# Selective-scan kernel: one scan instruction per unit, decays alternating between PSUM and SBUF, and work moved between the vector, scalar and GpSimd engines

## Chip, cores and metric

The kernel runs on one core of one Trainium2 chip. The metric is the device time of the whole program in microseconds (us). Lower is better. The engines are called as in the profile: PE is the matrix engine, PEld its weight loads, DVE the vector engine, ACT the scalar (activation) engine, POOL is GpSimd, and SP is the engine that issues most DMAs. PSUM is the memory that PE writes to, SBUF the larger on-chip memory. POOL's operations in this kernel read and write SBUF alone.

## What is computed

The input x is 8 images of 96 channels and 64 x 64 points, that is 8 sequences of 4096 tokens. Layer 0 is a selective-scan block with 192 inner channels and 16 states, layer 1 a linear attention and a feed-forward block with rounding to fp8 and fp16:

```python
u = group_norm(x)                                   # tokens x 96
xm, z = split(u @ in_proj_w.T)                      # 192 each
xm = silu(causal_conv4(xm) + conv_b)
dt, Bm, Cm = split(xm @ x_proj_w.T)                 # 6, 16, 16
delta = softplus(dt @ dt_proj_w.T + dt_proj_b)
dA  = exp(delta[..., None] * A)                     # channel x state
dBu = delta[..., None] * Bm[:, :, None, :] * xm[..., None]
h   = dA_t * h + dBu_t                              # over 4096 tokens, from h = 0
y   = sum_n(h * C_t) + xm * D
x   = x + layernorm((y * silu(z)) @ out_proj_w.T) * gamma + beta
t   = x + linear_attention(layernorm(x))            # 6 heads, no softmax
out = t + q16(q16(q8(relu_part) @ q8(W2).T) + q8(b2))
# relu_part = relu(q16(q16(q8(layernorm(t)) @ q8(W1).T) + q8(b1)))
```

Each channel and state is a linear recurrence over the tokens. Its factor is called the decay (dA), its addend dbu.

## The kernel before

**Tiling.** The images are taken in 4 pairs, the 4096 tokens in 8 chunks of T = 512, so there are 32 chunks in order. The 192 channels are 3 groups j of 64, the 16 states 4 groups g of 4. A tile of 128 partitions holds 4 states x 32 channels. A unit u (24 in a chunk) stands for one j, one g and one image b of the pair; its tile has two halves h (32 channels each) of 512 tokens side by side, hence 128 x 1024.

**A unit** (`unit`, L711) issues the following:
- the addend dbu of unit u + 3 (`products_b`, L656): POOL multiplies delta*u (du) by the rows of B, both in SBUF; four dbu buffers;
- two scans on DVE (L741), one for each half, each reading its decay from PSUM (tile da, one bank a half), dbu from SBUF and, as its start, the last state of the chunk before (tile state, one column per half; 0.0 in the first chunk of a pair);
- after each scan, the decay of the next unit's same half on ACT (`decay`, L675, Exp with a per-partition scale);
- the product with C: on DVE from PSUM (L763), where PE has spread the rows of C with a selection matrix (`rows_c`, L664, tile cc), or, for 6 units of the 24 (`POOLED`), on POOL (L770) from rows of C that DMAs have spread in SBUF (`rows`, L639, tile c);
- four matmuls per two units that add the products over the states (`sums`, L688, tile y);
- ACT's copy of the last state of each half (L719).

POOL has a product with C at units 4, 5, 12, 13, 20 and 21, all of g = 2.

**Around the units** run generators, whose steps the table `STEPS` (L37) puts at hand-chosen units, before ("part 0") or behind ("part 1") the scan: P (`chain_p`, the projections, Silu and Softplus of the chunk after next), E (`chain_e`, output projection and layer norms), G (group norm statistics of the next pair), W (attention weights of a pair), F0 and F1 (`chain_f`, the feed-forward block nine chunks later). The order written is the order of each engine's queue. At unit 10 (`SILU`) both decays of unit 12 are issued ahead into two other PSUM banks, mp and mE, just before the step of P that applies Silu to two tiles of 128 x 1536.

**Norms.** `norm_stats` (L399) gathers statistics on DVE (L406, L408); their ends are four small POOL operations (L412, L131, L132, L414: minus the mean, plus eps, the power -0.5, times), queued as "norms" and issued at the next unit's start. `normalise` (L418) applies them on ACT. The fp8 casts of the feed-forward block's hidden tiles are on POOL (L1011), queued as "others", issued behind the next scan.

**Activation tables.** Exp, Silu and Softplus need table loads on ACT; in a chunk there are four (1.28 us each).

**The tail.** After the last unit the remaining feed-forward chains run beside one another ("after" in `chain_f`); there DVE does the ReLUs (L1003) and bias adds that ACT does in the loop.

Of the kernel before, what the change touches and what calls it, by code (L numbers as in the profile page):

```python
# [24 lines left out]
POOLED = (4, 5, 12, 13, 20, 21)  # L25
POOLED_G = 2
SILU = 10
# [13 lines left out]
    3: "F1 F0 P | F1 G6",  # L41
    4: "| E",
# [23 lines left out]
def tile_mamba_linear_attention_ffn(  # L66
# [52 lines left out]

    def psum(tag="mp"):  # L120
        return ps_all.tile([128, T], F32, tag=tag, name=tag, bufs=2 if tag in ("cc", "da") else 1)
# [5 lines left out]
    nc.vector.memset(mhalf, -0.5)  # L127

# [270 lines left out]
    def norm_stats(src, n, tag):  # L399

        mv = p2.tile([128, n, 2], F32, tag=f"mv{tag}", name="mv")
        rstd = p2.tile([128, n], F32, tag=f"rs{tag}", name="rs")
        nmr = p2.tile([128, n], F32, tag=f"nm{tag}", name="nm")
        st = p1.tile([128, n, 6], F32, tag=f"st{tag}", name="st")
        for i in range(n):
            nc.vector.bn_stats(st[:, i, :], src[:, i, :])  # L406
        for i in range(n):
            nc.vector.bn_aggr(mv[:, i, :], st[:, i, :])  # L408


        def ends():
            nc.gpsimd.tensor_scalar_mul(nmr, mv[:, :, 0], -1.0)  # L412
            rsqrt(rstd, mv[:, :, 1], 1e-5)
            nc.gpsimd.tensor_mul(nmr, nmr, rstd)  # L414

        return rstd, nmr, later("norms", ends)

    def normalise(dst, src, norm, q):  # L418
        settle(norm[2])
        nc.scalar.activation(  # L420
            dst, src, AF.Identity, bias=norm[1][:, q : q + 1], scale=norm[0][:, q : q + 1]
        )
# [4 lines left out]
    def load_x(p, c):  # L427

        t = p1.tile([C, 2, T + 3], F32, tag="x", name="x")
        h = 3 if c else 0  # L430
        if not c:
            nc.gpsimd.memset(t[:, :, 0:3], 0.0)
        nc.sync.dma_start(
            t[:, :, 3 - h : T + 3],
            x[2 * p : 2 * p + 2, :, c * T - h : (c + 1) * T].rearrange("b c t -> c b t"),
        )
        x_next[p, c] = t

    def chain_p(p, c, s, after):
# [53 lines left out]
        nc.scalar.activation(zs, zs, AF.Silu)  # L493
        yield
# [26 lines left out]
        nc.scalar.activation(delta, delta, AF.Softplus)  # L521
        yield
# [18 lines left out]
    def first_p(s, after):  # L541
# [75 lines left out]

        cs = s["cs"] = p2.tile([128, T], F32R, tag="cs", name="cs")
# [3 lines left out]
        rows(s, "c", 2 * NS, POOLED_G)  # L622
# [16 lines left out]
    def rows(s, to, of, g):  # L639

        t = s[to, g] = p2.tile([128, 2, T], F32, tag=to, name=to, bufs=NG if to == "b" else 1)
        for n in range(NG):
            nc.sync.dma_start(
                t[32 * n : 32 * n + 32],
                s["bd"][of : of + 2 * NS].rearrange("(b n) t -> n b t", b=2)[NG * g + n]
# [4 lines left out]
    def rows_b(s, g):  # L650
        rows(s, "b", 0, g)
# [12 lines left out]
    def rows_c(s, u):  # L664
        j, g, b = where(u)
        if u in POOLED:
            return
# [7 lines left out]
    def decay(s, u, h, bank=None):  # L675
        if ("da", u, h) in s:
            return
        j, g, b = where(u)
        da = psum(bank) if bank else ps_all.tile([128, T], F32, tag="da", name="da", bufs=2)
        s["da", u, h] = da  # L680
        nc.scalar.activation(  # L681
            da, s["dl", j][:, 2 * b + h, :], AF.Exp, scale=aneg[:, 2 * j + h, g : g + 1]
# [28 lines left out]
    def unit(s, prev, nxt, first, u, steps):  # L711
# [4 lines left out]
        if u - 1 in POOLED:  # L716
# [11 lines left out]
        if u - 3 in POOLED and u % 2 == 0:  # L728
            sums(s, u - 3)
        if u % 2 == 0 and (u or prev is not None) and (u - 1) not in POOLED:  # L730
            sums(s if u else prev, (u or NU) - 1)
# [7 lines left out]
        to, v = at(u + 1)  # L739
        for h in range(2):  # L740
            nc.vector.tensor_tensor_scan(  # L741
                hs[:, h, :], s.pop(("da", u, h)), dbu[:, h, :],
                0.0 if first else state["last"][:, u, h : h + 1], ALU.mult, ALU.add,
            )
            if to is not None:
                decay(to, v, h)
# [7 lines left out]
        if u == SILU and (nxt is not None):  # L754
            for h in range(2):
                decay(s, u + 2, h, ("mp", "mE")[h])
# [3 lines left out]
        if u in POOLED:  # L760
            return
# [5 lines left out]
    def pooled(s, u):  # L767
        j, g, b = where(u)
        pr = s["pr", u] = p2.tile([128, 2, T], F32, tag="pq", name="pr")
        nc.gpsimd.tensor_mul(  # L770
            pr, s["hs", u], s["c", g][:, b, :].unsqueeze(1).to_broadcast([128, 2, T])
# [166 lines left out]
    def chain_f(p, c, b, banks, lane=None):  # L938
# [5 lines left out]
        def place(tag, out_tag, bufs):  # L944
# [5 lines left out]
            [128, NK, C], F32, name="x2", **place(f"x2{b}", ("pr", "b")[(lane or 0) % 2], 4)  # L950
# [34 lines left out]
        casts = []  # L985
# [13 lines left out]
        def relu(m):  # L999
# [6 lines left out]
            else:  # L1006
                nc.scalar.activation(h16[m], h16[m], AF.Relu, bias=b1q[:, m : m + 1])
            casts.append(
                later(
                    "others",  # L1010
                    lambda: nc.gpsimd.tensor_copy(h8[0][:, m, :], h16[m], saturate=False),  # L1011
                )
            )
# [15 lines left out]
        for job in casts:  # L1029
            settle(job)  # L1030
# [6 lines left out]
        y16 = p2.tile([C, T], F16, name="y16", **place("y16", "pq", 2))  # L1037
# [73 lines left out]
    waiting.update(norms=[], others=[])  # L1111
    with tc.manual_schedule():
        for u in range(AHEAD):
            products_b(slots[0], u)
        for h in range(2):
            decay(slots[0], 0, h)
        rows_c(slots[0], 0)
        for i, (p, c) in enumerate(chunks):
# [4 lines left out]
            def steps(u, part):  # L1123
                if part == 0:
# [6 lines left out]
                    if nxt is not None and u == NU - 1:  # L1131
                        rows(nxt, "c", 2 * NS, POOLED_G)
# [3 lines left out]
            for u in range(NU):  # L1136
                unit(s, prev, nxt, c == 0, u, steps)
# [4 lines left out]
    s = slots[N - 1]  # L1142
    sums(s, NU - 1)
# [83 lines left out]
```

## Time and profile before

Three runs give 3161.89, 3162.53 and 3166.35 us, the median is 3162.53. The profiled execution is one more; its page tells its span, from the first to the last instruction.

| What | Value |
|---|---|
| median of the runs | 3162.53 us |
| span of the profiled execution | 3160.5 us |
| first scan starts, last scan ends | 69.5 us, 3008.1 us |
| a chunk, later half of the run | 92.8 to 96.0 us |
| scans (L741) | 1536 of 128 x 512, 1205 to 1276 ns each |
| decays (L681) | 1536, 688 ns each |
| products for dbu (L659) on POOL | 768, 2371 ns each |
| products with C on DVE (L763), on POOL (L770) | 576 at 1213 ns, 192 at 2363 ns |
| ACT table loads | 128 in all |
| DMA | 443.75 MB, 140 GB/s |

Busy time is the time in which an engine works on an instruction. A group's row gives line, engine, operation, tiles and shapes, the count, the busy time, the mean length of one, then the idle time of the engine just ahead of them and what ended it. A recorded length runs until the instruction ends, and may hold time in which it was held up.

### The profile page before, as it was taken

To read this page: it belongs to the slowest core of one execution; us is meant where nothing else is said; L and a number is where in the kernel's file an instruction comes from. 1 tells how busy PE (TensorE), PEld (TensorE's weight loads), DVE (VectorE), ACT (ScalarE), POOL (GpSimd) and SP (SyncE) were. 2 spreads that over 40 slices of the span, in tenths; PEclk is the share of its full clock that TensorE was granted. 3 is DMA by queue.
4 is the path that set the end of the run, shared out by engine and by line. 5 is a ranking of instruction groups with operands and counts; after the bars stand their busy time and mean duration, and the time that the engine had idled before them with its cause. 6 is when DMAs were issued, how large, how long until landed. Compare 5 with 4: busy or idle time off the path is not lost. (4 is left out here: it accounts for less than half of the span.)

```text
span 3160.5 us, 35127 instructions
## 1 busy us (share of the span) xinstructions
PE 2469.6 (78%) x9450; PEld 928.7 (29%) x9450; DVE 2935.2 (93%) x4265; ACT 2263.9 (72%) x4360; POOL 2840.7 (90%) x1921
## 2 busy tenths in 40 slices
PE   6787787878787777777777778777888778887777
PEld 2122222222222223222233323222323222332344
DVE  4999999999999999999999999999999999999945
ACT  3666666667677777777777777777877777777656
POOL 2999999999999999999999999999999999999955
PEclk8677777787778888888888877898888888877668
DMA  6655556665555667555667555567565466755322
GB/s 149 152 122 137 134 156 152 160 150 135 141 143 135 138 162 175 146 129 125 141 164 170 141 146 125 137 157 170 146 148 127 124 144 162 169 132 134 95 70 73
DMA packets 253037, 443.75 MB, mean 140 GB/s; under 512 B 37605, under 2 KB 45990, under 8 KB 252838
## 3 DMA queue, kind: packets, MB, share of 16 engines
q1 hardware_dynamic: 247846, 439.40, 56.9%
q10 hardware_dynamic: 4992, 2.11, 0.3%
q8 instruction: 74, 1.21, 0.2%
q14 instruction: 125, 1.02, 0.1%
HBM read 349.11 MB, written 92.27 MB: 140 GB/s over the span
## 5 line engine op out<-in xcount | busy, mean ns | idle before, releaser
L659 POOL TENSOR_TENSOR dbu<-du,b 128x1024 f32<-128x1024 f32 x768 | 1804.6, 2371 | 112.6 <-DVE hs L741 65.5
L741 DVE TENSOR_TENSOR_SCAN hs<-da,state,dbu 128x512 f32<-128x512 f32 x1290 | 1573.5, 1265 | 25.6 <-ACT da L681 24.6
L681 ACT ACTIVATE da<-dl,aneg 128x512 f32<-128x512 f32 x1474 | 1000.6, 688 | 665.4 <-DVE hs L741 644.2
L763 DVE TENSOR_TENSOR pr<-hs,cc 128x1024 f32<-128x1024 f32 x576 | 698.7, 1213 | 35.1 <-DVE hs L741 0.5
L695 PE MATMUL y<-pr,ssum 128*32 128x512 f32 x2816 | 585.1, 831 | 113.3 <-DVE pr L763 113.3
L770 POOL TENSOR_TENSOR pr<-hs,c 128x1024 f32<-128x1024 f32 x192 | 453.8, 2363 | 36.6 <-DVE hs L741 30.4
L459 PE MATMUL mp<-u,wk 96*64 96x512 f32 x1488 | 398.1, 658 | 66.6 <-ACT xm L477 66.4
L671 PE MATMUL cc<-cs,sel 64*128 64x512 f32 x576 | 330.0, 583 | 144.8 <-DVE pr L763 144.4
L671 PEld LDWEIGHTS cc<-cs,sel 64*128 64x128 f32 x576 | 121.6, 215 | 557.3 <-DVE pr L763 296.8
L741 DVE TENSOR_TENSOR_SCAN hs<-da,dbu 128x512 f32<-128x512 f32 x184 | 213.2, 1205 | 17.4 <-POOL dbu L659 9.9
L516 PE MATMUL mp<-dbl,dtT 12*128 12x512 f32 x186 | 158.9, 947 | 56.8 <-ACT cs L506 38.5
L695 PEld LDWEIGHTS y<-pr,ssum 128*32 128x32 f32 x2816 | 87.9, 132 | 380.6 <-DVE pr L763 201.6
L791 PE MATMUL mE<-woT,zs 128*128 128x192 f32 x744 | 146.6, 350 | 66.7 <-ACT t1e L799 45.1
L459 PEld LDWEIGHTS mp<-u,wk 96*64 96x64 f32 x1488 | 97.0, 145 | 293.6 <-issue 156.6
L132 POOL TENSOR_TENSOR rs<-rs,mhalf 128x8 f32<-128x8 f32 (+1 forms) x128 | 173.3, 1354 | 10.7
L791 PEld LDWEIGHTS mE<-woT,zs 128*128 128x128 f32 x744 | 127.3, 200 | 126.8 <-ACT t1e L799 70.5
L703 PE MATMUL y<-xm,dd 128*128 128x512 f32 x192 | 129.2, 760 | 22.4 <-DVE zs L709 21.9
L467 PE MATMUL mp<-u,wz 96*64 96x512 f32 x372 | 137.0, 825 | 4.3 <-ACT xm L485 4.3
L1011 POOL CAST h<-h 128x512 fp8e5<-128x512 f16 x192 | 117.6, 622 | 24.8 <-DVE h L1003 15.8
L719 ACT COPY state<-hs 128x2 f32<-128x2 f32 x736 | 130.1, 181 | 0.2
L420 ACT ACTIVATE o<-x,nm,rs 128x96 f32<-128x96 f32 x256 | 98.6, 455 | 36.4 <-POOL nm L414 34.4
L531 POOL TENSOR_TENSOR du<-delta,xm 128x512 f32<-128x512 f32 x93 | 117.1, 1273 | 0.0
(306 smaller groups left out, 3234.1 us busy)
## 6 DMA issues: line engine op xcount, KB each, us to landing
du<-lu SPq DMA_DIRECT2D x380, 256.0 KB, 5.5
dl<-ld SPq DMA_DIRECT2D x380, 256.0 KB, 7.9
b<-bd SPq DMA_DIRECT2D x512, 128.0 KB, 5.0
lu<-du SPq DMA_DIRECT2D x96, 256.0 KB, 5.7
ld<-delta SPq DMA_DIRECT2D x93, 256.0 KB, 2.4
c<-bd SPq DMA_DIRECT2D x128, 128.0 KB, 4.4
xg<-in_x_dram SPq DMA_DIRECT2D x32, 384.0 KB, 3.8
xr<-in_x_dram SPq DMA_DIRECT2D x32, 384.0 KB, 8.7
```

What stands on the lines that cost most here:

```text
L132: nc.gpsimd.tensor_tensor(out_, out_, mhalf[0 : out_.shape[0], 0 : out_.shape[1]], op=ALU.pow)
L459: nc.tensor.matmul(ps[64 * b : 64 * b + 64, :], lhsT=wk[:, k, 64 * j : 64 * j + 64], rhs=u[:, b, k : k + T], start=(k == 0), stop=(k == 3),)
L467: nc.tensor.matmul(ps[64 * b : 64 * b + 64, :], lhsT=wz[:, 64 * j : 64 * j + 64], rhs=u[:, b, 3 : T + 3], start=True, stop=True,)
L516: nc.tensor.matmul(ps, lhsT=dtT[:, j, :], rhs=dbl[0 : 2 * RANK, :], start=True, stop=True)
L659: nc.gpsimd.tensor_mul(dbu, s["du", j][:, 2 * b : 2 * b + 2, :], s["b", g][:, b, :].unsqueeze(1).to_broadcast([128, 2, T]),)
L671: nc.tensor.matmul(cc, lhsT=sel[64:128, g, b], rhs=s["cs"][64:128, :], start=True, stop=True)
L681: nc.scalar.activation(da, s["dl", j][:, 2 * b + h, :], AF.Exp, scale=aneg[:, 2 * j + h, g : g + 1])
L695: nc.tensor.matmul(s["y"][q : q + 32, :], lhsT=ssum, rhs=pr[:, h, :], start=False, stop=(g == NG - 1),)
L741: nc.vector.tensor_tensor_scan(hs[:, h, :], s.pop(("da", u, h)), dbu[:, h, :], 0.0 if first else state["last"][:, u, h : h + 1], ALU.mult, ...
L763: nc.vector.tensor_mul(pr, hs, s.pop(("cc", u)).unsqueeze(1).to_broadcast([128, 2, T]))
L770: nc.gpsimd.tensor_mul(pr, s["hs", u], s["c", g][:, b, :].unsqueeze(1).to_broadcast([128, 2, T]))
L791: nc.tensor.matmul(ps[:, 2 * k * C : 2 * (k + 1) * C], lhsT=zs[:, j, tok : tok + 128], rhs=woT[:, j].rearrange("p b c -> p (b c)"), start= ...
```

## The change

The diff does the following:
1. **One scan per unit** of 128 x 1024 over both halves. The decays of a unit lie side by side in one tile; the decay at the start of half 1 is 0 (column written once, left out by the Exp: `h:T`), and ACT puts the carried state into the addend there: dbu[:, 1, 0] += a0 * last (`carry`, one column, pointer scale and bias). The first decays a0 are four more two-column Exps for each j and chunk (`first_decays`). Neither is done in the first chunk of a pair.
2. **Two decay tiles**: even units use PSUM (da, two banks), odd units an SBUF tile (ds). Decays are issued two units ahead, behind the scan of the unit that used the tile. The ahead-of-Silu decays in mp and mE are gone.
3. **Norms**: the four POOL operations become Ln(var + eps) and Exp(-0.5 ...) on ACT and one DVE operation for minus mean times root ("shifts", issued behind the scan). `exp_and_ln()` loads one table that has both, after Silu and after Softplus.
4. **fp8 casts** go to ACT in the loop; in the tail they stay on POOL.
5. **POOL's products with C**: 9 units of 24 instead of 6 (u % 8 in 0, 2, 5), each with its own tile of C rows (64 KB DMAs, 12 a chunk instead of 4 of 128 KB), loaded at units 20, 22 and 1; their results share the ring of four pr tiles. The sums are issued at u % 8 = 3, 5 and 0 (twice).
6. One step of F0 moves from unit 3 to unit 4.

```diff
-POOLED = (4, 5, 12, 13, 20, 21)
-SILU = 10
+POOLED = (0, 2, 5)
+ROWS_POOLED = {20: (0, 0), 22: (1, 0), 1: (2, 1)}
-    3: "F1 F0 P | F1 G6",
-    4: "| E",
+    3: "F1 P | F1 G6",
+    4: "| F0 E",
...
+    das = [
+        ps_all.tile([128, 2, T], F32, tag="da", name="da"),
+        const.tile([128, 2, T], F32, name="ds"),
+    ]
...
-        def ends():
-            nc.gpsimd.tensor_scalar_mul(nmr, mv[:, :, 0], -1.0)
-            rsqrt(rstd, mv[:, :, 1], 1e-5)
-            nc.gpsimd.tensor_mul(nmr, nmr, rstd)
+        def power():
+            nc.scalar.activation(rstd, mv[:, :, 1], AF.Ln, bias=eps5)
+            nc.scalar.activation(rstd, rstd, AF.Exp, scale=-0.5)
+        def shift():
+            nc.vector.scalar_tensor_tensor(
+                nmr, mv[:, :, 0], -1.0, rstd, ALU.mult, ALU.mult
+            )
...
+    def decay(s, u):
         j, g, b = where(u)
+        for h in range(2):
+            nc.scalar.activation(
+                das[u % 2][:, h, h:T], s["dl", j][:, 2 * b + h, h:T], AF.Exp,
+                scale=aneg[:, 2 * j + h, g : g + 1],
+            )
+    def first_decays(s, j):
+        a0 = s["a0", j] = p2.tile([128, NG, 2], F32, tag="a0", name="a0")
+        dl = s["dl", j].rearrange("p (b h) t -> p b h t", h=2)
+        for g in range(NG):
+            nc.scalar.activation(
+                a0[:, g, :], dl[:, :, 1, 0], AF.Exp, scale=aneg[:, 2 * j + 1, g : g + 1]
+            )
+    def carry(s, u, last):
+        j, g, b = where(u)
+        if not u % (2 * NG):
+            first_decays(s, j)
+        to = s["dbu", u][:, 1, 0:1]
         nc.scalar.activation(
+            to, s["a0", j][:, g, b : b + 1], AF.Identity, bias=to, scale=last[:, u, 1:2]
         )
...
-        for h in range(2):
-            nc.vector.tensor_tensor_scan(
-                hs[:, h, :], s.pop(("da", u, h)), dbu[:, h, :],
-                0.0 if first else state["last"][:, u, h : h + 1], ALU.mult, ALU.add,
-            )
-            if to is not None:
-                decay(to, v, h)
+        if u + 1 < NU:
+            if not first:
+                carry(s, u + 1, state["last"])
+        elif nxt is not None and not last:
+            carry(nxt, 0, state["new"])
+        nc.vector.tensor_tensor_scan(
+            hs.rearrange("p h t -> p (h t)"),
+            das[u % 2].rearrange("p h t -> p (h t)"),
+            dbu.rearrange("p h t -> p (h t)"),
+            0.0 if first else state["last"][:, u, 0:1], ALU.mult, ALU.add,
+        )
+        to, v = at(u + 2)
+        if to is not None:
+            decay(to, v)
+        now("shifts")
         now("others")
...
-        if u in POOLED:
+        if u % 8 in POOLED:
             return
...
-            casts.append(
-                later(
-                    "others",
-                    lambda: nc.gpsimd.tensor_copy(h8[0][:, m, :], h16[m], saturate=False),
-                )
-            )
+            if after:
+                nc.gpsimd.tensor_copy(h8[0][:, m, :], h16[m], saturate=False)
+            else:
+                nc.scalar.activation(h8[0][:, m, :], h16[m], AF.Copy, saturate=False)
```

## The prediction

> **What bounds the kernel now.** I read the busy times first, then the stretch in which the scans run (first scan at 69.5 us, last end at 3008 us), then the waits.
>
> ```profile
> PE 2469.6 (78%) x9450; PEld 928.7 (29%) x9450; DVE 2935.2 (93%) x4265; ACT 2263.9 (72%) x4360; POOL 2840.7 (90%) x1921
> ```
>
> ```profile
> 69.00:3005.00 2936.00, 2311.26 (x8796) 838.61 (x8796) 2829.49 (x3874) 2149.80 (x4113) 2742.39 (x1722) 0.81 0.59 144
> ```
>
> ```profile
> ACT da L681 <- DVE hs L741: 644.2, 820, 4.0
> ...
> POOL dbu L659 <- DVE hs L741: 65.5, 66, 2.6
> ...
> DVE hs L741 <- ACT da L681: 31.7, 43, 1.2
> ```
>
> The second fence is the table of busy times by stretch: length, then PE, PEld, DVE, ACT, POOL. In these 2936 us DVE works 2829 (96.4%), POOL 2742 (93.4%), ACT 2150 (73%). The waits agree: ACT waits 644 us for scans, POOL 65 us, the scans hardly for anyone. DVE bounds, POOL is 3% behind. The chain that ended last covers only some 1% of the span (the tail) and says nothing of the loop. Outside this stretch lie 3160.5 - 2936 = 224.5 us. My sums are made against the span of 3160.5; the median of the runs is 3162.5, so I add 2 at the end.
>
> **The rows that price the parts** (by form: shapes, count | busy, mean ns).
>
> ```profile
> L659 POOL TENSOR_TENSOR dbu<-du,b 128x1024 f32<-128x1024 f32 x768 | 1804.6, 2371 | 112.6 <-DVE hs L741 65.5 <-DMA ld<-delta 36.9 <-DMA dl<-ld 4.6
> L741 DVE TENSOR_TENSOR_SCAN hs<-da,state,dbu 128x512 f32<-128x512 f32 x1290 | 1573.5, 1265 | 25.6 <-ACT da L681 24.6
> L763 DVE TENSOR_TENSOR pr<-hs,cc 128x1024 f32<-128x1024 f32 x576 | 698.7, 1213 | 35.1 <-DVE hs L741 0.5
> L770 POOL TENSOR_TENSOR pr<-hs,c 128x1024 f32<-128x1024 f32 x192 | 453.8, 2363 | 36.6 <-DVE hs L741 30.4 <-DMA xr<-in_x_dram 3.6 <-DMA xg<-in_x_dram 1.4
> L709 DVE TENSOR_TENSOR zs<-y,zs 128x512 f32<-128x512 f32 x96 | 64.2, 668 | 5.4 <-PE y L695 4.7
> L132 POOL TENSOR_TENSOR rs<-rs,mhalf 128x8 f32<-128x8 f32 x64 | 106.8, 1670 | 5.3
> ```
>
> *One scan of 1024 for two of 512.* A pair costs 1573.5/1290 x 2 = 2.44 us of DVE. A longer scan is not in the trace. At worst nothing is gained: 2.44. What doubling saves is one fixed part: the products show it, 2 x 668 (L709) - 1213 (L763) = 123 ns; the pointer start (scans with state 1259, without 1199 at the median) may save another 60: 2.26. I take 2.30, near the 123 ns: 768 x 0.14 = -107 us on DVE.
>
> *Products with C.* 96 move (288 instead of 192 on POOL): DVE -96 x 1.213 = -116, POOL +96 x 2.36 = +227. PE loses 96 spreads of C (L671), which bound nothing.
>
> *Norms.* A norm on POOL is four operations: L412 257, L131 248, L132 1670, L414 205 ns at 8 columns (2.38 us), 1.73 us at 4. Of the 128 norms some 21 lie in the tail; the others take 226 us from POOL. DVE gets one small operation each (L186 is like it, 130 ns): +14. ACT gets Ln and Exp: about 0.28 and 0.18 us (L681 less its 512 columns; the small copy L719, 181 ns), 107 x 0.46 = +49. Both lie in one table, and by the instruction order the table loads stay 63 + 31 + 31: no new load.
>
> *Casts.* 138 go to ACT at L997's 578 ns: +80 there; 132 of them, in the loop, leave POOL: -132 x 0.612 = -81.
>
> *Carry.* 672 one-column operations with pointer scale and bias: L420 takes 455 ns for 96 columns; at the 0.79 ns a column of 674 (512) to 1483 (1536) it is 0.38 us, so +255. 336 first decays of two columns: 0.28 us, +95. ACT in all: 2150 + 479 = 2629.
>
> *Waits on ACT.* A carry waits for POOL's product of the same unit; behind it in ACT's queue stand the decays of the unit after, copies and norms, and the scans wait for them. POOL runs up to three units ahead, which covers it; where POOL is late, the scan waits for that product anyway, so it adds nothing. And a carry stands behind Silu with its loads (1.28 + 1.48 + 1.47 + 1.28 = 5.5 us). Before, both decays of unit 12 were made ahead in two spare banks; now, after unit 10's scan, ACT does two decays (1.4), Silu (5.5), state and carry (0.6): 7.5 us, while DVE has one scan, one product and some 0.5 to do (4.0). That is up to 3.5 us a chunk, 31 x 3.5 = 108 us, on DVE if DVE has no other wait.
>
> *Rows of C.* 12 loads of half the size for 4 a chunk, on SP, which waits 463 us in all for one chain alone. They are issued four to five units (15 us and more) ahead of their readers, c landed in 4.4 us; their old readers are POOL products three units back. Nothing waits behind them: 0. The later sums are 8 short matmuls a chunk-third instead of 4 ahead of the gate, under a scan of 2.3 us: 0.
>
> Without anything else DVE comes to 2829 - 107 - 116 + 14 = 2620, POOL to 2742 + 227 - 226 - 81 = 2662, ACT to 2629: three level engines.
>
> **The port.** What the sum leaves out is where the decays lie. They alternate between PSUM (even units) and an SBUF tile "ds" (odd units). An odd scan then streams both operands from SBUF; no scan of before does (its POOL neighbours never stretch: L659 2338 to 2452 ns). How DVE and POOL can meet in SBUF, the trace shows in three places (timeline: start, us, operation):
>
> ```profile
> 606.12 2.36 POOL L659 TENSOR_TENSOR dbu<-du,b 128x1024 f32<-128x1024 f32 x1 [1.96 <-DMA dl<-ld]
> ...
> 606.50 2.00 DVE L170 COPY gnm<-gnmv 96x2 f32<-96x2 f32 x1
> ...
> 608.42 1.21 DVE L763 TENSOR_TENSOR pr<-hs,cc 128x1024 f32<-128x1024 f32 x1
> ```
>
> ```profile
> 3032.07 0.61 POOL L1011 CAST h<-h 128x512 fp8e5<-128x512 f16 x1 [0.92 <-DVE h L1003]
> ...
> 3032.24 0.58 DVE L1003 TENSOR_SCALAR h<-h,b1q 128x512 f16<-128x512 f16 x1
> ```
>
> ```profile
> 622.08 1.67 POOL L132 TENSOR_TENSOR rs<-rs,mhalf 128x8 f32<-128x8 f32 x1
> ...
> 622.88 0.16 DVE L176 TENSOR_TENSOR gndev<-gnm,gnmean 96x2 f32<-96x2 f32 x1
> ```
>
> A copy of two columns, 165 ns when POOL is idle, lasts 2.00 us and ends 0.02 us after the POOL product at 608.48; its two later sisters in the loop also end with a POOL product. L1003 (330 ns alone) ends 0.14 us behind POOL's cast. So DVE and POOL can shut each other out for a whole instruction. The third fence is the other bound: operations with two SBUF inputs passed beside POOL's power unhindered (nine of nine). But L1003 passes beside the power too (0.35 us at 3071.13, inside a power of 1.04 us from 3071.09), so that operation keeps nobody out, and the nine tell little. No long POOL operation meets a two-input DVE operation in this trace: what an odd scan costs POOL lies between 0 and its full length. Its neighbours are POOL's long products, as in the first fence, so I take the exclusive end as the nearest row, and POOL pays: 384 x (2.30 + 0.03) = 895; the 107 norm shifts, two SBUF inputs too, 107 x 0.16 = 17. POOL with what it is shut out: 2662 + 895 + 17 = 3574 us. DVE waits for half a POOL product (1.2) per odd scan or shift: 2620 + 491 x 1.2 = 3209, so it has room, and the 108 us behind Silu fit into it. At a bound engine's share between 96.4% (now) and 100%, 98%: 3647; + 224.5 + 2 = **3874, say 3870 us**. With 2.26 a scan and 100% it is 3785; with 2.44 and 96.4%, 3990.
>
> A rule speaks to just this. The Trainium skill, "SBUF — State Buffer", section "Who interferes with whom", says that a DVE instruction with two SBUF inputs contends with a GpSimd instruction that reads SBUF, through the shared read interface, and that the loser blocks fully. By it the sum is the 3870 above; by the third fence alone, taken as the rule's counterexample, it would be the 3050 below. No run here shows it for a scan.
>
> **The rivals.**
> *No contention.* Then the change is faster: DVE 2620 + 108 behind Silu = 2728, POOL 2662. At 96.4%: 2830 + 224.5 + 2 = **3055** (3000 to 3155, as three level engines with ACT one unit ahead may reach less). It decides from the price of an odd scan on POOL: the loop keeps its 2936 us when POOL holds 0.98 x 2936 = 2877, that is (2877 - 2662)/384 = 0.56 us a scan; below that the change is faster, above it slower. For it: L176 to L178; against: L170, L1003.
> *Port shared, not locked.* Both read at once and slow one another; half the exclusive price, 448: POOL 3110 / 0.97 = 3206, **3430** (3160 to 3780).
> *ACT becomes the bound without contention.* 2629 at 88% (waits for scan, product and Silu in one queue): 2988 + 227 = **3215**, on the slow side by a little. In the level state this needs ACT to lose 12%; now it loses 27%, but for lack of work.
> *The scan doesn't shrink.* At 2.44 a scan DVE has 107 more: 3055 becomes 3160; under the lock it adds 54 (384 x 0.14).
>
> **How the numbers follow.** Lock 0.68, shared 0.11, no contention and faster 0.17, ACT-bound or level 0.04 (of which within 0.2%: 0.02). 0.2%, some 6 us, is about what a measurement of this kernel can tell from no change. Faster 0.17, same 0.02, slower 0.81. The lock's own range is 3785 to 3990, with 0.65 of chance. To hold 8 in 10 the range takes in the shared port and the slow ACT case and leaves out the faster one: 3160 to 3990.
>
> **What would show it.** Lock: POOL products of du and b stretched to 4 us and more, or DVE scans on ds with a recorded time far above those on da; POOL's busy share near 100%; ACT and DVE idle behind dbu. No lock: all these products stay at 2.37 us and scans of both tiles at 2.3. Silu: scan of unit 12 late by some 3 us in each chunk. I am wrong if both scan forms take the same 2.3 us beside unstretched POOL products.

## The result, and the profile after

The changed kernel takes 3689.23 us (median of four runs, 3686.88 to 3692.76), the kernel before on the same chip 3162.21 us (four runs): a ratio of 1.166, interval 1.1646 to 1.1679. The profiled execution spans 3687.5 us. The forecast was 3870 us, the range 3160 to 3990.

The busy times of the changed kernel:

```profile
PE 2676.0 (73%) x9610; PEld 1039.6 (28%) x9610; DVE 3336.0 (90%) x3532; ACT 2658.3 (72%) x5762; POOL 3417.5 (93%) x1367
```

The table by stretch, from its first scan (72.3 us) to the end of its last (3558.7 us); the columns are the stretch, its length, PE, PEld, DVE, ACT and POOL:

```profile
72.00:3558.00 3486.00, 2531.97 (x8970) 962.33 (x8970) 3230.01 (x3119) 2535.99 (x5469) 3362.17 (x1261) 0.72 0.50 124
```

POOL works 3362 of these 3486 us (96.4%, before 93.4%), DVE 3230 (92.7%, before 96.4%). DVE executes fewer instructions than before and is still busy for 400 us more, so part of its "busy" must be waiting inside instructions. The groups show where:

```profile
L689 POOL TENSOR_TENSOR dbu<-du,b 128x1024 f32<-128x1024 f32 x768 | 2195.7, 2879 | 60.7 <-DMA du<-lu 36.8
L793 DVE TENSOR_TENSOR_SCAN hs<-ds,state,dbu 128x1024 f32<-128x1024 f32 x336 | 1135.3, 3379 | 28.6 <-ACT dbu L728 24.7
L823 POOL TENSOR_TENSOR pr<-hs,c 128x1024 f32<-128x1024 f32 x288 | 852.6, 2961 | 73.2 <-DVE hs L793 35.0
L793 DVE TENSOR_TENSOR_SCAN hs<-da,state,dbu 128x1024 f32<-128x1024 f32 x336 | 786.1, 2339 | 70.6 <-ACT dbu L728 61.0
...
L728 ACT ACTIVATE dbu<-a,dbu,state 128x1 f32<-128x1 f32 x672 | 255.9, 381 | 70.9 <-POOL dbu L689 70.7
...
L428 DVE SCALAR_TENSOR_TENSOR nm<-mv,rs 128x8 f32<-128x8 f32 (+1 forms) x128 | 154.1, 1204 | 40.4 <-ACT rs L425 39.2
```

The even scans, which read their decay from PSUM (da), take 2339 ns. The odd ones have the same shape and count and read it from SBUF (ds): 3379 ns. The kernel's granted TensorE clock is lower too (0.72 against 0.81 in the stretch of the scans), but that cannot be what makes the odd scans longer: the even ones run at the same clock. POOL's product for dbu has grown from 2371 to 2879 ns, its product with C from 2363 to 2961 ns. A carry costs 381 ns. The shift of the norms (L428), a few columns wide, takes 1204 ns. The timeline shows what a meeting of the two engines looks like, in two places, and at the end a scan on da for comparison (start, length, operation):

```profile
1499.64 6.66 POOL L689 TENSOR_TENSOR dbu<-du,b 128x1024 f32<-128x1024 f32 x2
1499.73 4.41 DVE L793 TENSOR_TENSOR_SCAN hs<-ds,state,dbu 128x1024 f32<-128x1024 f32 x1
...
1518.58 2.32 DVE L793 TENSOR_TENSOR_SCAN hs<-ds,state,dbu 128x1024 f32<-128x1024 f32 x1
...
1518.80 4.26 POOL L823 TENSOR_TENSOR pr<-hs,c 128x1024 f32<-128x1024 f32 x1 [1.25 <-DVE hs L793]
...
1523.02 2.34 POOL L689 TENSOR_TENSOR dbu<-du,b 128x1024 f32<-128x1024 f32 x1
...
1523.17 2.35 DVE L793 TENSOR_TENSOR_SCAN hs<-da,state,dbu 128x1024 f32<-128x1024 f32 x1 [0.56 <-ACT dbu L728]
```

First the scan begins 0.09 us behind a product and lasts 4.41 us, until 1504.14: it is held while the product runs, then takes its 2.3 us, and the second product behind it is held in turn (6.66 us for two that need 4.7). In the second place the scan is first by 0.22 us; it takes 2.32 us, and the product, held until about the scan's end, takes 4.26 us. The last two lines show a scan on da beside a product: neither is longer than its group's usual 2.34 and 2.36 us.

Summed over the trace, POOL's operations in this stretch are 698 us longer than their undisturbed lengths (dbu 403, products with C 174, the rest 121), that is 1.82 us for each of the 384 odd scans; a product that is stretched at all is stretched by 2.0 us for dbu and 1.7 for C. The odd scans are 405 us longer than even ones. Without these, POOL has 3362 - 698 = 2664 us of work.

The waits of the changed kernel (who waited for whom: us in all, times, longest) carry little beside that (ACT waits most, for scans, and is not the bound at 72%):

```profile
ACT ds L708 <- DVE hs L793: 411.3, 216, 7.5
...
ACT dbu L728 <- POOL dbu L689: 70.7, 84, 3.1
...
DVE hs L793 <- ACT dbu L728: 85.7, 92, 3.4
DVE nm L428 <- ACT rs L425: 39.2, 28, 2.1
```

Of the 85.7 us that scans wait for the carry, 48 lie at unit 12, behind Silu (24 of 32 chunks, 2.0 us each).

### The profile page after: what moved, and what is told of

Same layout as the page of the kernel before. It is cut to its first block, busy times and chain, and to the rows that moved or that the text cites. A ratio compares the mean times of both kernels' runs of the same rounds, so it can differ in the third digit from the quotient of the medians.

```text
span 3687.5 us, 35488 instructions
## 1 busy us (share of the span) xinstructions
PE 2676.0 (73%) x9610; PEld 1039.6 (28%) x9610; DVE 3336.0 (90%) x3532; ACT 2658.3 (72%) x5762; POOL 3417.5 (93%) x1367
## 5 line engine op out<-in xcount | busy, mean ns | idle before, releaser
L689 POOL TENSOR_TENSOR dbu<-du,b 128x1024 f32<-128x1024 f32 x768 | 2195.7, 2879 | 60.7 <-DMA du<-lu 36.8
L793 DVE TENSOR_TENSOR_SCAN hs<-ds,state,dbu 128x1024 f32<-128x1024 f32 x336 | 1135.3, 3379 | 28.6 <-ACT dbu L728 24.7
L823 POOL TENSOR_TENSOR pr<-hs,c 128x1024 f32<-128x1024 f32 x288 | 852.6, 2961 | 73.2 <-DVE hs L793 35.0
L793 DVE TENSOR_TENSOR_SCAN hs<-da,state,dbu 128x1024 f32<-128x1024 f32 x336 | 786.1, 2339 | 70.6 <-ACT dbu L728 61.0
L708 ACT ACTIVATE da<-dl,aneg 128x512 f32<-128x512 f32 (+1 forms) x768 | 529.3, 689 | 390.0 <-DVE hs L793 358.9
L708 ACT ACTIVATE ds<-dl,aneg 128x512 f32<-128x512 f32 (+1 forms) x768 | 511.2, 713 | 412.4 <-DVE hs L793 411.3
L816 DVE TENSOR_TENSOR pr<-hs,cc 128x1024 f32<-128x1024 f32 x480 | 581.5, 1212 | 25.9 <-DVE hs L793 0.9
L728 ACT ACTIVATE dbu<-a,dbu,state 128x1 f32<-128x1 f32 x672 | 255.9, 381 | 70.9 <-POOL dbu L689 70.7
L428 DVE SCALAR_TENSOR_TENSOR nm<-mv,rs 128x8 f32<-128x8 f32 (+1 forms) x128 | 154.1, 1204 | 40.4 <-ACT rs L425 39.2
L793 DVE TENSOR_TENSOR_SCAN hs<-ds,dbu 128x1024 f32<-128x1024 f32 x48 | 166.1, 3460 | 11.0 <-POOL pr L823 7.8
```

The costliest lines, as they stand in the source:

```text
L689: nc.gpsimd.tensor_mul(dbu, s["du", j][:, 2 * b : 2 * b + 2, :], s["b", g][:, b, :].unsqueeze(1).to_broadcast([128, 2, T]),)
L708: nc.scalar.activation(das[u % 2][:, h, h:T], s["dl", j][:, 2 * b + h, h:T], AF.Exp, scale=aneg[:, 2 * j + h, g : g + 1],)
L728: nc.scalar.activation(to, s["a0", j][:, g, b : b + 1], AF.Identity, bias=to, scale=last[:, u, 1:2])
L793: nc.vector.tensor_tensor_scan(hs.rearrange("p h t -> p (h t)"), das[u % 2].rearrange("p h t -> p (h t)"), dbu.rearrange("p h t -> p (h t) ...
L816: nc.vector.tensor_mul(pr, hs, s.pop(("cc", u)).unsqueeze(1).to_broadcast([128, 2, T]))
L823: nc.gpsimd.tensor_mul(pr, s["hs", u], s["c", g, b].unsqueeze(1).to_broadcast([128, 2, T]))
```

## The experiments

Times are medians; a ratio is to the kernel before, in runs on the same chip. Theory L is the prediction's: DVE and POOL shut each other out whenever a scan reads both operands from SBUF. Its rivals are that new waits in the queues make the time, or that DVE bounds anyway. Other letters hold within one text only.

**1. The lock by itself.** Pairs of a DVE and a GpSimd operation, by themselves. Tile pa lies in PSUM, all others in SBUF; the two stretches below stand for seven.

```diff
+        for _ in range(N):
+            nc.vector.tensor_tensor_scan(h, pa, b, 0.0, ALU.mult, ALU.add)
+            nc.gpsimd.tensor_mul(r, p, q)
+        fence()
+        for _ in range(N):
+            nc.vector.tensor_tensor_scan(h, a, b, 0.0, ALU.mult, ALU.add)
+            nc.gpsimd.tensor_mul(r, p, q)
...
```

> The kernel leaves the whole computation out and writes constants; it only runs stretches of twelve pairs, one DVE and one GpSimd operation at 128x1024 that share no data. Theory L (the lock: a DVE operation whose two operands both lie in SBUF and a GpSimd operation that reads SBUF shut each other out for whole instructions): the scan from PSUM beside the GpSimd product keeps 2.3 us and the product 2.36 us; the scan with both operands in SBUF beside the product makes a pair of 4.5 to 4.8 us (12 pairs in about 56 us); beside a GpSimd memset, which reads nothing, it keeps 2.3 us; beside a GpSimd multiplication by a constant, which reads one operand, it is shut out as well; a DVE product of two SBUF operands is shut out like the scan (pair of some 3.6 us), a DVE product from PSUM is not (2.36 us); the operation of 8 columns waits for the end of the product each time (2.0 to 2.4 us recorded). Rival S (the port is shared, both run slower at once): pairs of 2.4 to 4 us with both operations stretched, and the 8-column operation takes well below 1 us. Rival N (the long scans of the changed kernel are slow for another reason, say dependences): every pair takes the longer of its two, about 2.4 us.

The groups of this kernel by shape, costliest first. Pairs stand on neighbouring lines: L136 with L137, L140 with L141, and so on; p, q, a, b are in SBUF, pa in PSUM:

```profile
L141 POOL TENSOR_TENSOR r<-p,q 128x1024 f32<-128x1024 f32 x12 | 50.7, 4221 | 0.9
L140 DVE TENSOR_TENSOR_SCAN h<-a,b 128x1024 f32<-128x1024 f32 x12 | 49.0, 4083 | 0.4
L153 POOL TENSOR_TENSOR r<-p,q 128x1024 f32<-128x1024 f32 x12 | 38.6, 3219 | 0.9
L152 DVE TENSOR_TENSOR h<-a,b 128x1024 f32<-128x1024 f32 x12 | 36.9, 3075 | 0.4
L149 POOL TENSOR_SCALAR r<-p 128x1024 f32<-128x1024 f32 x12 | 36.7, 3055 | 1.0
L148 DVE TENSOR_TENSOR_SCAN h<-a,b 128x1024 f32<-128x1024 f32 x12 | 34.6, 2886 | 0.4
L161 POOL TENSOR_TENSOR r<-p,q 128x1024 f32<-128x1024 f32 x12 | 28.2, 2346 | 0.9
L157 POOL TENSOR_TENSOR r<-p,q 128x1024 f32<-128x1024 f32 x12 | 28.1, 2343 | 0.9
L137 POOL TENSOR_TENSOR r<-p,q 128x1024 f32<-128x1024 f32 x12 | 28.1, 2340 | 0.9
...
L144 DVE TENSOR_TENSOR_SCAN h<-a,b 128x1024 f32<-128x1024 f32 x12 | 27.5, 2290 | 0.4
...
L136 DVE TENSOR_TENSOR_SCAN h<-pa,b 128x1024 f32<-128x1024 f32 x12 | 27.5, 2290 | 0.4
L156 DVE TENSOR_TENSOR h<-pa,b 128x1024 f32<-128x1024 f32 x12 | 14.7, 1223 | 0.4
L160 DVE SCALAR_TENSOR_TENSOR h<-a,b 128x8 f32<-128x8 f32 x12 | 14.2, 1180 | 0.4
L145 POOL MEMSET r<- 128x1024 f32 x12 | 11.4, 951 | 0.7
```

Beside the scan from PSUM (L136) the product keeps 2340 ns, as alone (2338); beside the same scan from SBUF (L140) both become 4.1 to 4.2 us long. So the effect needs no other part of the kernel, and rival N falls. That it is a lock and not a port shared at half speed (S) shows in the shortest and longest of a group (ns: shortest, median, longest):

```profile
L140 DVE TENSOR_TENSOR_SCAN h<-a,b x12: 2278/4246/4250, 124.4 to 169.5; 128x1024 f32<-128x1024 f32 x12
...
L160 DVE SCALAR_TENSOR_TENSOR h<-a,b x12: 154/1180/2195, 312.5 to 324.8; 128x8 f32<-128x8 f32 x12
```

The first SBUF scan, which starts with the first product (within 0.01 us), takes 2.28 us as alone, and that product 4.42; the 8-column operations take up to 2.19 us. A memset, which reads nothing, is no partner (L144). A DVE product of two SBUF operands is shut out like the scan (L152). A GpSimd operation that reads one operand makes the scan 0.6 us longer (L148, 2886 ns); how long that operation (L149) takes alone was not run, so whether the two shut each other out for the whole length, as was expected, is not shown. But two exclusive operations would need 2.29 + 2.34 = 4.63 us a pair and take 4.22: some 0.4 us overlap, and POOL loses 4.22 - 2.34 = 1.88 us a scan, not 2.33. The 8-column operation takes 1180 ns on average: every second one waits to the end of the product (2.19 us), the next passes in 0.17, and POOL loses nothing.

**2. The place of the operand alone.** The kernel before, two scans of 512 kept, with the decays of odd units in SBUF.

```diff
-        da = psum(bank) if bank else ps_all.tile([128, T], F32, tag="da", name="da", bufs=2)
+        if u % 2:
+            da = p2.tile([128, T], F32, tag="ds", name="ds", bufs=2)
+        else:
+            da = psum(bank) if bank else ps_all.tile([128, T], F32, tag="da", name="da", bufs=2)
```

POOL's results go through the ring of DVE's here too, to make room.

> The kernel before, with one thing changed: the decays of the odd units lie in SBUF, those of the even units stay in PSUM. There are still two scans of 512 a unit; norms, casts and the six products on GpSimd stay (the latter's results use the ring of the other products, which makes room). Theory L (an odd scan reads two SBUF streams and shuts GpSimd out, and waits for it): GpSimd's 2742 us in the loop grow by 768 half scans x 1.26 us x 0.78 (the share that the changed kernel showed: 698 us for 384 scans of 2.33) = 755; 3497 at 96.4% and 222 outside: 3850 us, 3500 to 3900; products on GpSimd stretched in bundles. Rival W (GpSimd or ScalarE simply got too much work in the change): no work moves here, so 3160, within 15.

3963.43 us, ratio 1.253 (1.251 to 1.2547): moving the operand alone costs 800 us against the kernel before on the same chip (3163.75 us), more than the whole change. Its page, the busy times and three groups:

```profile
PE 2843.6 (72%) x9450; PEld 1014.3 (26%) x9450; DVE 3724.6 (94%) x4265; ACT 2242.4 (57%) x4360; POOL 3339.1 (84%) x1921
...
L659 POOL TENSOR_TENSOR dbu<-du,b 128x1024 f32<-128x1024 f32 x768 | 2021.1, 2644 | 313.6 <-DVE hs L744 274.1
L744 DVE TENSOR_TENSOR_SCAN hs<-ds,state,dbu 128x512 f32<-128x512 f32 x672 | 1497.5, 2267 | 15.7 <-ACT ds L684 14.6
...
L744 DVE TENSOR_TENSOR_SCAN hs<-da,state,dbu 128x512 f32<-128x512 f32 x618 | 755.6, 1263 | 0.0
```

A half scan on ds takes 2267 ns instead of 1263: 768 x 1.004 = 771 us of waiting on DVE, which is 94% busy and bounds. POOL loses 498 us (3339 - 2841). That scans and products hold each other up, as L says, holds; but L laid the loss on POOL (755 us more), and here it is DVE that loses most and bounds. Its range (up to 3900) was too low, because each of the 768 half scans can wait anew. A half scan waits as long as a whole one does in the changed kernel (1.0 and 1.05 us), so here the price on DVE goes by the number of meetings, not by the length.

**3. One scan a unit alone.** The kernel before with the long scan, the carry and ds (parts 1 and 2 of the change, with the step of F0 that moves); norms, casts and 6 of 24 products as before, their results in the ring of DVE's.

```diff
+        nc.vector.tensor_tensor_scan(
+            hs.rearrange("p h t -> p (h t)"),
+            das[u % 2].rearrange("p h t -> p (h t)"),
+            dbu.rearrange("p h t -> p (h t)"),
+            0.0 if first else state["last"][:, u, 0:1], ALU.mult, ALU.add,
+        )
...
```

> The kernel before with the one scan per unit alone (decays in PSUM and SBUF by turns, carries and first decays on ScalarE); norms, casts and six products stay on GpSimd. Theory L: GpSimd's 2742 us grow by 384 x 1.8 = 700; 3440 at 96.4% and 222 outside: 3790, 3650 to 3850 us. If the loss came from the other parts: 3060 to 3200.

3791.08 us, ratio 1.196 (1.1943 to 1.1979). Its busy times:

```profile
PE 2796.0 (74%) x9450; PEld 1008.4 (27%) x9450; DVE 3309.0 (87%) x3499; ACT 2520.9 (67%) x5368; POOL 3586.9 (95%) x1921
```

POOL goes from 2840.7 to 3586.9 us of busy time, 746 more, 1.94 us for each odd scan, and is 95% busy; L's number is met. The part alone costs 623 us against the kernel before on the same chip (3168.53 us), more than all parts together (527).

**4. Everything but the one scan.** The changed kernel with two scans of 512, decays in PSUM and the ahead-of-Silu decays, as before.

```diff
-        nc.vector.tensor_tensor_scan(
-            hs.rearrange("p h t -> p (h t)"),
...
+        for h in range(2):
+            nc.vector.tensor_tensor_scan(
+                hs[:, h, :], s.pop(("da", u, h)), dbu[:, h, :],
+                0.0 if first else state["last"][:, u, h : h + 1], ALU.mult, ALU.add,
+            )
+            if to is not None:
+                decay(to, v, h)
...
```

> The changed kernel with two scans of 512 a unit and all decays in PSUM as before; norms and casts on ScalarE, nine of 24 products on GpSimd. Theory L: no long stretch; GpSimd 2664, DVE 2829 - 116 + 107 norm shifts x (0.13 + up to 1 of waiting) = 2750 to 2840; at 96.4% and 205 outside: 3060 to 3150, faster than before by 0.5 to 3%. Rival W: GpSimd overloaded by the products as in the change, 3500 or more.

3339.94 us, ratio 1.055 (1.0529 to 1.0569). No stretched product (POOL's dbu 2364 ns), and yet 190 us above what was expected. So the scans on ds are not the whole loss: the other parts are slower by themselves, by 176 us against the 527 of the whole change. Three waits of it:

```profile
POOL pr L793 <- PE y L715: 127.0, 50, 5.1
POOL dbu L679 <- DVE hs L763: 115.0, 61, 3.6
DVE nm L418 <- ACT rs L415: 109.4, 54, 2.8
```

DVE waits 109 us for roots at the head of its queue, where before none of these was; the shift itself has 77.2 + 48.7 = 126 us for 128 operations that need 0.13 us each. POOL waits 127 us for the sums that free the ring of four.

**5. Norms alone, with the shift on DVE and on GpSimd.** The kernel before with Ln and Exp on ACT. In the second version the shift stays on GpSimd:

```diff
-            nc.vector.scalar_tensor_tensor(
-                nmr, mv[:, :, 0], -1.0, rstd, ALU.mult, ALU.mult
-            )
+            nc.gpsimd.tensor_scalar_mul(nmr, mv[:, :, 0], -1.0)
+            nc.gpsimd.tensor_mul(nmr, nmr, rstd)
```

> The kernel before with the norms alone changed: roots as Exp of Ln on ScalarE, the shift as one DVE operation with two SBUF inputs. Theory S: each of some 107 shifts in the loop costs DVE about 1 us at the port and 0.9 us of waiting for ScalarE's roots: DVE 2829 + 200; 3250 to 3380 us. By the prediction's price without waits (14 us on DVE, GpSimd 226 less): 3150 to 3180.

> The kernel before with the norms' roots on ScalarE (Ln, Exp) and their two small operations left on GpSimd: the norms' part of the change without the shift on DVE, everything else as before. Moving the norms with the shift on DVE measured 3260 us, 97 more than before. Theory S (the price lies in the shift: an operation at the head of DVE's queue that waits for a root in ScalarE's queue, and for GpSimd's port): without it DVE, 2829 us of work, bounds as before: 3155 to 3175 us, GpSimd down to some 2560. Rival Q (the price lies in ScalarE's queue, where decays now stand behind roots that wait for DVE's statistics): it stays at 3210 to 3260, with scans waiting for decays.

3259.79 us, ratio 1.0283 (1.0267 to 1.0298), with the shift on DVE; 3157.65 us, ratio 0.998 (0.9972 to 0.999), with it on GpSimd. The group of the shift, from the page of the version with the shift on DVE:

```profile
L418 DVE SCALAR_TENSOR_TENSOR nm<-mv,rs 128x8 f32<-128x8 f32 (+1 forms) x128 | 90.6, 708 | 31.8 <-ACT rs L415 31.8
```

Two waits of the version with the shift on GpSimd:

```profile
POOL nm L419 <- ACT rs L415: 51.9, 38, 2.7
...
DVE hs L753 <- ACT da L693: 34.1, 46, 2.1
```

One small operation on the bound engine, 128 times, costs about 100 us (102 by the two medians, 96 by the two ratios). The first fence accounts for them: 90.6 us in which the 128 shifts hold DVE, where 128 x 0.13 = 17 were priced, and 31.8 us of idle time ahead of them, waiting for a root: 74 + 32 = 106. That they last 708 ns on average (1146 at 8 columns) agrees with the 8-column pairs of experiment 1 (1180). With the shift on GpSimd the wait for the root (51.9 us) falls on POOL, which has the room. The roots on ACT cost nothing (34 us of scans waiting for decays, 32 before), and POOL's 205 us less work (2635.6 against 2840.7) is worth about 6 us, since DVE bounds. This version is faster than both kernels, than the one before by 0.2%.

The same swap in the version of experiment 4:

> The kernel with all of the change but the one scan, and the norm shift made by two GpSimd operations (minus the mean, times the root) instead of one DVE operation. Theory S: DVE loses the 218 us of waiting of that kernel's 3340, GpSimd gains 50: 3060 to 3180 us, at or below before. Rival Q (the ring of four result tiles, for which GpSimd waited 127 us there, or the order of the queues bounds): 3280 to 3350.

3259.32 us, ratio 1.0284 (1.0254 to 1.0313), 81 us less than with the shift on DVE. It lies between the two ranges of the text, a little under Q's. Here scans wait 130 us for ACT's decays and POOL 116 us for the sums, so the shift is one part of what was missed in experiment 4. The queue of ACT and the ring are, by these waits, the rest; neither was tried alone.

**6. Products alone, and a version without two SBUF reads on DVE's long operations.** The first is the kernel before with the 9 of 24 products. The second is the last version of experiment 5 (3259.32 us) with 8 products of 24, a ring of five, and the casts on GpSimd again; the lines below leave out those of the casts:

```diff
-POOLED = (0, 2, 5)
+POOLED = (0, 2, 5, 8, 13, 16, 18, 21)
...
-        pr = s["pr", u] = p2.tile([128, 2, T], F32, tag="pr", name="pr", bufs=4)
+        pr = s["pr", u] = p2.tile([128, 2, T], F32, tag="pr", name="pr", bufs=5)
...
```

> The kernel before with one part of the change alone: three of eight products with C on GpSimd, spread, with own tiles for the rows of C; the norms, casts and both scans a unit stay as before. By the terms of the prediction GpSimd gets 96 x 2.36 = 227 us more, 2742 + 227 = 2969, and becomes the bound: at 96.4% to 100% 2969 to 3080 + 224.5 = 3190 to 3305 us; DVE falls to 2713. Rival R (the ring of four results that GpSimd and DVE now share, with sums three units later, adds waits of DVE on the sums): DVE and GpSimd both below 93% busy and above 3330 us. If GpSimd were not the bound: 3050 us.

> A version that keeps what pays: two scans of 512 from PSUM as before (no decays in SBUF), the norms' roots on ScalarE with their shift on GpSimd, casts on GpSimd again, eight products of 24 with C on GpSimd, in a ring of five. By the rows DVE has 2829 - 64 x 1.213 = 2751 us, GpSimd 2742 + 151 - 180 = 2713, ScalarE 2150 + 49 = 2199: if the engines keep the level of before, 2751/0.964 + 222 = 3076 us. If the waits that the version of nine products showed come from the ring of four and from the casts in ScalarE's queue, it comes to 3060 to 3150. Rival Q: the waits come from the roots in ScalarE's queue (decays stand behind a root that waits for DVE's statistics); then it stays at 3200 to 3280, above the kernel before.

3318.82 us, ratio 1.0486 (1.047 to 1.0501), and 3201.33 us, ratio 1.0118 (1.0101 to 1.0135). The products alone make POOL the bound, a little above the top of the expected 3305: of the 3096 us from 69 to 3165 POOL works 2961 (95.6%). The second is 58 us better than the last version of experiment 5 but 50 above what was expected, just inside Q's range. Its waits:

```profile
POOL pr L792 <- DVE hs L762: 87.9, 67, 2.3
...
POOL dbu L678 <- DVE hs L762: 69.7, 84, 3.6
DVE hs L762 <- ACT da L700: 66.8, 56, 4.8
DVE gram L890 <- PE mE L881: 62.2, 20, 3.6
```

DVE at 90% and POOL at 87% wait for each other, for ACT's decays and for PE in turn, none for long. Since three edits went into it together, it doesn't tell which of them gave the 58 us.

**7. Two of eight products on POOL.** The changed kernel with one product of each eight back on DVE:

```diff
-POOLED = (0, 2, 5)
-ROWS_POOLED = {20: (0, 0), 22: (1, 0), 1: (2, 1)}
+POOLED = (0, 5)
+ROWS_POOLED = {20: (0, 0), 1: (2, 1)}
...
```

> The changed kernel with two of eight products with C on GpSimd instead of three (units 0 and 5 of each eight). Theory L with GpSimd as the bound: its loop of 3362 loses 96 x 2.36 = 227, 3135 at 96.4% and 201 outside: 3450 us (3420 to 3520), still far above before. Rival A (ScalarE's queue, the carries behind Silu, is what bounds): unchanged, 3690 within 20. Rival D (DVE, with its waits at the port, bounds): slower, by 96 x 1.21 = 116, some 3800.

3603.93 us, ratio 1.1398 (1.1379 to 1.1417). Its busy times:

```profile
PE 2664.9 (74%) x9706; PEld 1048.1 (29%) x9706; DVE 3268.6 (91%) x3628; ACT 2652.4 (74%) x5762; POOL 2925.9 (81%) x1271
```

It fits none of the three. 96 products fewer are 227 us less for POOL and 116 more for DVE; the time falls by 85. POOL is 81% busy, DVE 91%, the odd scans take 3031 ns instead of 3379. So a loop in which POOL bounds alone does not describe it. One reading is that under the lock neither engine bounds alone: what one gives up the other partly takes by running into it. No run tests that reading by itself.

**8. Taking the lock out of the changed kernel: two tries that brought waits of their own.** The first has three PSUM banks for the decays, for which C's spread rows keep one bank instead of two and the decays come later. The second lets odd scans read one zero column of PSUM instead of ds. Their edits, one behind the other:

```diff
-    das = [
-        ps_all.tile([128, 2, T], F32, tag="da", name="da"),
-        const.tile([128, 2, T], F32, name="ds"),
-    ]
+    da3 = ps_all.tile([128, 3, T], F32, tag="da", name="da")
+    das = [da3[:, 0:2, :], da3[:, 1:3, :]]
...
-        cc = s["cc", u] = ps_all.tile([128, T], F32, tag="cc", name="cc", bufs=2)
+        cc = s["cc", u] = ps_all.tile([128, T], F32, tag="cc", name="cc", bufs=1)
...
```

```diff
-            das[u % 2].rearrange("p h t -> p (h t)"),
+            das[0][:, 1, 0:1].to_broadcast([128, 2 * T])
+            if u % 2 else das[0].rearrange("p h t -> p (h t)"),
```

> The changed kernel with all decays in PSUM: three banks side by side, even units in banks 0 and 1, odd units in banks 1 and 2; the spread rows of C have one bank instead of two. One decay of the next unit can start only after the scan, and ScalarE has one small copy more per even unit (a zero in the shared bank). Theory L: GpSimd's products go back to 2.36 us each, its loop to 2664, DVE to some 2640 plus waits for the late decay (up to 0.8 us in 3 of 8 units): 3050 to 3250 us. Rival W (too much work on GpSimd or ScalarE): the work is the same and ScalarE has 75 us more, so 3690 or more.

> The changed kernel; its odd scans read, in place of the decays in SBUF, one zero column of PSUM repeated 1024 times, so the recurrence of the odd units is left out. ScalarE still makes those decays, every instruction of every queue stays, and only the odd scan's second SBUF stream is gone. Theory L (the two-stream scan shuts GpSimd out): scans of both kinds 2.3 us, GpSimd's products 2.36 us each, but for the norm shifts; its loop back to some 2680. With L alone as the loss, 3050 to 3150; with theory S beside it (the norm shift on DVE waits for ScalarE's roots and at the port, as the kernel without the one scan showed: 3340), 3150 to 3350. If the port is not the cause: 3690.

3758.57 us, ratio 1.188 (1.1863 to 1.19), and 3498.49 us, ratio 1.104 (1.102 to 1.1057). In both the stretching of products and scans is gone (POOL's dbu 2358 and 2363 ns, scans of even and odd units some 2345), but both are slow for a reason that is not in the changed kernel. Two waits of the first:

```profile
ACT da L710 <- DVE hs L793: 476.0, 298, 4.4
DVE hs L793 <- ACT da L710: 434.2, 418, 3.8
```

And one of the second:

```profile
DVE hs L793 <- ACT da L708: 252.9, 252, 2.4
```

The first makes a circle of decay and scan, in which each waits for the other 434 and 476 us. In the second the zero column belongs to the tile da, so odd scans wait for the next even unit's decays (253 us). For theory L both expectations missed. The first time lies where its rival W put it (3690 or more), but not for W's reason of too much work: POOL and ACT are 73% busy. The two versions show that the stretching comes from ds, and don't give the time of a changed kernel without the lock.

## Why the prediction was right, and what in it was not

- **The range held with some luck.** The lock's own range, 3785 to 3990, was missed from below: 3689 lies in the range that the prediction gave for a shared port (3160 to 3780), and only the whole range took both in. So the time alone does not tell a lock from a shared port; the timelines and experiment 1 do.
- **The lock** was the likeliest case, and holds: with the operand in PSUM no product is stretched (experiments 1, 4 and 8), with it in SBUF they are, and its place alone costs 800 us (2). The rule of the Trainium skill that the prediction weighed ("SBUF — State Buffer", section "Who interferes with whom") agrees with the rows of experiment 1 in who meets whom: of the DVE operations there only those with two SBUF inputs, and only beside a POOL operation that reads. That the loser waits out the whole instruction holds there beside a POOL product, but for 0.3 to 0.4 us, and is open beside the POOL operation with one operand. Experiment 1 has no copy; in the first fence of the prediction's part on the port a copy with one SBUF input is held as well (2.00 us), so two inputs are not the only case. The third fence there, the nine small operations that passed beside the power, did not decide it; why they passed was not tried.
- **The shut-out was mis-sized**: 895 + 17 us on POOL in the prediction (2.33 us a scan, 0.16 a shift), 698 measured (1.82 a scan, shifts included). Experiment 1 shows 1.88 us a scan for POOL, since about 0.4 us of each pair overlap, and a shift costs POOL nothing. This is the largest error: (912 - 698)/0.98 = 218 us.
- **POOL without shut-outs**: 2662 predicted, 2664 measured. One scan of 1024: 2.30 predicted, 2.34 (da) measured. The carry: 255 and 256 us. First decays: 95 and 72 us.
- **POOL's share** was taken as 98% and is 96.4% (+57 us), and outside the loop lie 201 us, not 224.5 (-24). With -218 these make the 185 us between 3874 and 3689.
- **DVE** was put at 3209 us with its waits and has 3230, but the step "so it has room" was too easy: at 92.7% it isn't a free engine beside a bound POOL. What the prediction named as a sign of the lock, ACT and DVE idle behind dbu, is small (71 us for ACT), and in experiment 7 227 us less for POOL bring only 85.
- **Norms at +14 us on DVE** held for the work alone. Under the lock the prediction gave each shift 1.2 us of waiting, and the row has 1.20 with the work. What it lacked is that this wait, and the one for the root, come without long scans on ds too: about 100 us alone (5), 81 in the version of experiment 4.
- **Silu**: up to 3.5 us a chunk predicted, 2.0 us in 24 of 32 chunks measured, 48 us in all.
- **No contention, 3055 us**, the rival on the faster side: its term DVE + 108 leaves out the shift, the ring of four and ACT's queue. Without the lock the other parts alone are at 3340 us (4), and with the shift off DVE at 3259. Whether one scan without the lock would bring that below 3162 stays open, as neither try of experiment 8 was clean. That the later sums cost 0 holds under the lock (POOL waits 24 us for them), not without it (127 us in experiment 4).
- **Not additive**: one scan alone +623, everything else alone +176, together +527. The rest moves work so that POOL's plain load falls by about 80 us (2742 to 2664) and DVE's by 116; that is worth little in the kernel before, where only DVE's counts, and may be worth more where both engines hold each other up. This reading fits experiments 3, 4 and 7; no run isolates it.

## What to carry to other kernels

Before an operand of a DVE operation moves from PSUM to SBUF, look for what GpSimd does beside it: with both operands in SBUF the two engines hold each other up, at about 1 us of waiting for DVE and 1.8 to 1.9 for GpSimd for each long scan here. Price a small operation on the bound engine by what it waits for (a mean of 0.7 to 1.2 us here, not 0.13). Where two engines are both 90% busy, compare the mean length of one operation on two tiles: busy time can be waiting inside instructions.

## What the runs showed of the hardware that was not expected

- The turns are not wholly exclusive: a scan and a product of 2.29 and 2.34 us make a pair of 4.22, a product and a product of 1.22 and 2.34 one of 3.22, so 0.3 to 0.4 us overlap.
- A DVE operation of 8 columns with two SBUF operands takes up to 2.19 us beside GpSimd's product in experiment 1 and costs GpSimd nothing (2346 against 2338 ns).
- It need not get its turn behind one product. In the changed kernel a group norm's operation of two columns with two SBUF operands (L198) takes 7.92 us, three times in the loop, and 0.16 us where GpSimd is idle. It waits for the end of the product that it meets and for three more that follow without a gap:

```profile
765.79 4.67 POOL L689 TENSOR_TENSOR dbu<-du,b 128x1024 f32<-128x1024 f32 x2
...
767.16 7.92 DVE L198 SCALAR_TENSOR_TENSOR gnnmr<-gnmean,gnrstd 96x2 f32<-96x2 f32 x1
...
770.40 2.36 POOL L823 TENSOR_TENSOR pr<-hs,c 128x1024 f32<-128x1024 f32 x1
772.71 2.35 POOL L689 TENSOR_TENSOR dbu<-du,b 128x1024 f32<-128x1024 f32 x1
```

  In experiment 4 five of the 128 shifts outlast a product in this way, the longest at 5.73 us. No odd scan of the changed kernel takes more than 4.57 us, that is, waits for more than one product. Why a small operation can be passed over and a scan was not is open.
- A GpSimd memset is neither held nor holds (951 ns each, the scan 2290), while a GpSimd operation with one SBUF operand holds the scan for 0.6 us (2886 ns).
